# A third set of expert weights in the attention's matrices, list entries asked for three blocks ahead, half gathers behind half blocks

## The chip, the cores and the metric

The kernel runs on one core of one Trainium2 chip. A core has five engines with their own instruction streams: TensorE (PE, the matrix unit, with its weight loads PEld), VectorE (DVE), ScalarE (ACT), GpSimd (POOL) and SyncE (SP, which here issues most of the plain transfers). Sixteen DMA engines move data between the device memory and the on-chip memory. The metric is the device time of one execution in microseconds (us), as a median over several runs.

## The reference, cut to what matters

The input x has shape (4, 1024, 256): 4096 tokens of 256 features. Each token passes a gated scan layer (the "attention") and then a mixture of experts, both inside an adaptive layer norm. All data are float32.

```python
h = layernorm(x) * (1 + ca) + sa
x = x + ga * attn(h)            # K, u, g_in, g_out = sigmoid/linear parts of xn @ W_K, xn @ W_ugg;
                                # scan over the sequence; (outputs * g_out) @ W_out, plus h
h = layernorm(x) * (1 + cb) + sb
scores = top2(softmax(h @ Wg + bg))              # 8 experts, 2 per token, renormalised
for e in range(8):                               # W1[e]: 256 x 1024, W2[e]: 1024 x 256
    y = gelu(h @ W1[e] + b1[e]) @ W2[e] + b2[e]
    out += y * weight_of_expert_e
x = x + gb * out
```

## The kernel before

**First part, the attention.** The tokens go through in eight chunks of 512 (`for c_ in range(NCH)`). For each chunk `project` is called four times (`hc` 0 to 3); each call makes four products with slices of `wk_sb` and `wu_sb` (the tiles `pk`, `pgi`, `pu`, `pgo`, line 411). W_K, W_ugg and W_out lie in on-chip memory in the tiles `wk_sb`, `wu_sb` and `wo_sb` for the whole run. `wo_sb` is read by `scale_out` only, at the start of a sequence. Inside the last `project` call of the last chunk, between the products `pgi` and `pu`, stands `b_turn(0)`: PE turns the rows of the first expert block (tile `ptx`, line 878).

**The lists.** In between the chunks the gate's choices are sorted: for each token and chosen expert a pair (token, weight) is scattered into a list in device memory (`lists`, line 580). Each expert's list is cut into blocks of 256 tokens (`TK`); a table of block number to expert and place is computed on the chip: `tab["e"]` for the first eight blocks (`NE`), which are made from the first half of the tokens alone, and `tab["l"]` for the others. The blocks that have over 128 tokens ("whole") come first and those with at most 128 ("half") last. How many there are of either depends on the data, so the last blocks stand in branches: `n_whole` and `n_blocks` are read from the chip. In this run 36 blocks are used: 31 whole ones, then 5 half ones. In what follows they are named by their number: 30 is the last whole block, 31 to 35 are the half ones.

**Second part, the blocks.** For a block `j` the kernel does:

- `fetch_entries(j)`: SP reads the block's place from the table and loads its entries (`ente` for the first eight, `ent` in four turns for the others, 2 KB, line 808).
- `fetch_rows(j)`: POOL gathers the rows of the tokens from `hx` in device memory into `hb` (three turns), in two indirect transfers of 128 rows of 2 KB (line 820).
- `fetch_weights(j)`: SP loads `w1` (1 MB), `bb`, `w2` (1 MB) and `b2b` (128 KB) of the expert, in two turns each (lines 837 to 840).
- `b_turn(j)`: DVE turns `hb` into `xT` by sixteen 32-row transposes (line 885).
- `b_up(j)`: PE makes `ph` from `w1` and `xT` (line 898), ACT the gelu `g` (line 907).
- `b_down(j)`: PE makes `pye` from `g` and `w2` (line 928); DVE adds `b2b` and multiplies by weight and gate (lines 942, 943); POOL adds the result to the output in device memory by an indirect accumulating transfer (line 915).

From block 31 on the last result of a block is kept back: it goes to the one tile `last_y` with its places copied into the one tile `last_at` (line 938), and is sent by `add_rows` at the start of the next block's branch (`rest`, line 1160). So block j+1 may write `last_at` only when the transfer of block j has landed.

**The order.** It is written out by hand (`manual_schedule`): every engine runs its instructions in program order. `fetch(j)`, called at the start of block j, asks for the rows of block j+2 (and, from block 8 on, its entries just ahead of them) and for the weights of block j+1. `fetch_used(j)` does the same with a branch around each of the two, and stands ahead of the branch on `n_whole`. The first weights and all eight early entries are asked for in the last chunk:

```python
if not more:
    fetch_weights(0)
    for j in range(NE):
        fetch_entries(j)
    wait_for(BK[0]["ld"], scattered)
    fetch_rows(0)
    fetch_rows(1)
```

The weights of block 1 follow after the chunk loop, in `fetch(0)`.

Transfers that SP issues use eight completion counters in turn, and a transfer that takes a counter waits for the one that had it before.

Of the kernel before, what the change touches and what calls it, by code (L numbers as in the profile page):

```python
# [9 lines left out]
F32 = mybir.dt.float32  # L10
I32 = mybir.dt.int32
# [8 lines left out]
def tile_adaln_block(  # L20
# [33 lines left out]
    P = 128  # L54
    B, S, D = x.shape
    H = W_out.shape[0]
    E, _, F = W1.shape
    T = B * S
    KC = D // P
    HC = H // P  # L60
    FC = F // P
# [6 lines left out]
    HK = TK // P  # L68
# [5 lines left out]
    NJ = (2 * T + E * (TK - 1)) // TK  # L74
    BPE = T // TK
    NE = 8
# [13 lines left out]
    apool = ctx.enter_context(tc.tile_pool(name="attn", bufs=1))  # L90
# [3 lines left out]
    xpool = ctx.enter_context(tc.tile_pool(name="blocks", bufs=2))  # L94
# [11 lines left out]
        )  # L106
    )

    wk_sb = apool.tile([P, KC, H], F32, tag="wk", name="wk_sb")
    wu_sb = apool.tile([P, KC, 3 * H], F32, tag="wu", name="wu_sb")  # L110
    wo_sb = apool.tile([P, HC, D], F32, tag="wo", name="wo_sb")

    kts = [
# [120 lines left out]
    def a_norm(c_):  # L234
        X[c_]["h"] = deep.tile([P, TPB, D], F32, tag="h", name=f"h_{c_}")
        norm(X[c_]["h"], c_)
# [235 lines left out]
    def f_norm(c_):  # L472
        norm(new_h2(c_), c_)
# [301 lines left out]
    BK, tab = {}, {}  # L775
# [3 lines left out]
    def turns(pool, n: int, shape, dtype, tag: str, j: int):  # L779

        slots = kept.setdefault(tag, [None] * n)
        if slots[j % n] is None:
            slots[j % n] = pool.tile(shape, dtype, tag=f"{tag}{j % n}", name=f"{tag}_{j % n}", bufs=1)
        return slots[j % n]
# [6 lines left out]
    def seen(j: int):  # L791
        return EARLY_B * S if j < NE else T
# [8 lines left out]
    def fetch_entries(j: int):  # L801
        at = entry(j, 1, E * BPE)
        if j < NE:
            ent = xpool.tile([P, HK, 2], I32, tag=f"ente{j}", name=f"ente_{j}", bufs=1)
        else:
            ent = turns(xpool, 4, [P, HK, 2], I32, "ent", j)
        with nc.allow_non_contiguous_dma(reason="pairs of a list"):
            ld = nc.sync.dma_start(out=ent, in_=by_block[at])
        BK.setdefault(j, {}).update(ent=ent, ld=ld, gathers=[], acc=[])

    def fetch_rows(j: int):

        if j >= NJ:
            return
        if j >= NE:
            fetch_entries(j)
        hb = turns(xpool, 3, [P, HK, 2 * D], F32, "hb", j)
        for t in range(HK):
            BK[j]["gathers"].append(
                nc.gpsimd.indirect_dma_start(  # L820
                    out=hb[:, t, :], out_offset=None, in_=hx[: seen(j), :],
                    in_offset=IndirectOffsetOnAxis(ap=BK[j]["ent"][:, t, 0:1], axis=0),
                    bounds_check=seen(j) - 1, oob_is_err=False,
                )
            )
        BK[j]["hb"] = hb

    def fetch_weights(j: int):
        if j >= NJ:
            return  # L830
        wpool = pools["w"]
        e = entry(j, 0, E - 1)
        w1 = turns(wpool, 2, [P, KC, F], F32, "w1", j)
        w2 = turns(wpool, 2, [P, FC, D], F32, "w2", j)
        bb = turns(wpool, 2, [P, FC], F32, "bb", j)
        b2b = turns(wpool, 2, [P, D], F32, "b2b", j)
        nc.sync.dma_start(out=w1, in_=W1r[e])
        nc.sync.dma_start(out=bb, in_=b1d[e])
        nc.sync.dma_start(out=w2, in_=W2r[e])
        nc.sync.dma_start(out=b2b, in_=b2[ds(e, 1), :].broadcast_to((P, D)))  # L840
        BK.setdefault(j, {}).update(w1=w1, w2=w2, bb=bb, b2b=b2b)

    def fetch(j: int):

        fetch_rows(j + 2)
        fetch_weights(j + 1)

    def fetch_used(j: int):


        def used(i: int, step):
            if i < sure:
                step(i)
            elif i < NJ:
                with tc.If(n_blocks > i):
                    step(i)

        used(j + 2, fetch_rows)
        used(j + 1, fetch_weights)

    def wait_for(ins, others):
        for other in others:
# [3 lines left out]
                reason="all of it is there",  # L866
            )

    def b_turn(j: int):


        xT = turns(xpool, 2, [P, KC, TK], F32, "xT", j)
        BK[j]["xT"] = xT
        if j == 0:
            pt = ps_tr.tile([P, KC, TK], F32, tag="tr", name=f"ptx_{j}")
            for k in range(KC):
                for t in range(HK):
                    nc.tensor.transpose(pt[:, k, ts(t, P)], BK[j]["hb"][:, t, ts(k, P)], ident)
            nc.vector.tensor_copy(xT, pt)
            return  # L880
        hb = BK[j]["hb"][:, :, :D].rearrange("p t (k c) -> p t k c", k=KC)
        to = xT.rearrange("p k (t n) -> p t k n", t=HK)
        for i in range(NQ):
            for q in range(NQ):
                nc.vector.transpose(to[ts(q, SQ), :, :, ts(i, SQ)], hb[ts(i, SQ), :, :, ts(q, SQ)])  # L885
# [78 lines left out]
    h = X[0]["h"]  # L964
# [25 lines left out]
    for c_ in range(NCH):  # L990
        nxt, prv, old = c_ + 1, c_ - 1, c_ - 2
        more, was, been = nxt < NCH, prv >= 0, old >= 0
        b, part = divmod(c_, NB)

        route = old // NB if been and old % NB == NB - 1 else None
        placed = (c_ - 3) // NB if c_ >= 3 and (c_ - 3) % NB == NB - 1 else None


        if c_ + 3 < NCH:
            load_x(c_ + 3, nc.sync)  # L1000
        if more:
            shift(nxt)
        project(c_, 0, [lambda: a_norm(nxt)] if more else [])
        drain(6)
        if more:
            a_mod(nxt)
        if was:
            a_skip(c_)
            o_pe(prv)
            o_resid(prv)  # L1010
        if placed is not None:
            r_second(placed)
        if part == NB - 1:
            load_mdf(b + 1)


        if part == 0 and was:
            scale_out(b)
        if was:
            f_stats(prv)  # L1020
        project(c_, 1, [lambda: a_square(nxt)] if more else [])
        if c_ == 0:
            first_contents()
        drain(6)
        if placed is not None:
            r_rank_pe(placed)
        if been:
            f_gate(old)
        if not more:
            fetch_weights(0)  # L1030
            for j in range(NE):
                fetch_entries(j)

# [3 lines that stand above are left out]
        if part == 0:  # L1037
            if c_ == 0:
                setup_ctx.close()
                pools["w"] = ctx.enter_context(tc.tile_pool(name="weights", bufs=2))  # L1040
            load_gb(b)
            load_mda(b + 1)
        elif c_ == 1:
            clear_rows()
            if c_ == 0:
                load_mdf(1)


        if more:
            a_root(nxt)  # L1050
        if was:
            shift(prv)
        if placed is not None:
            r_place(placed)
        if route is not None:
            r_softmax(route)
        if more:
            a_scale(nxt)
        project(
            c_, 2,  # L1060
            ([lambda: f_norm(prv)] if was else [])
            + ([lambda: r_exp(route)] if route is not None else []),
        )
        drain(6)
        if part == 0:
            store_gb(b)
        if c_ + 2 < NCH:
            a_stats(c_ + 2)


        if not was:
            a_skip(c_)
            scale_out(b)
        if was:
            f_mod(prv)
            f_store(prv)
        project(c_, 3, [lambda: a_turn(nxt) if more else b_turn(0)])
        drain(6)
        if was:
            f_swap(prv)  # L1080
        if route is not None:
            r_first(route)
        if placed == EARLY_B - 1:
            tab["e"] = early_table()
# [35 lines left out]
    tab["l"], ends_at = late_table()  # L1120

    def work(j: int, half: bool = False, keep: bool = False):
        b_up(j, half)
        if j + 1 < NJ:
            b_turn(j + 1)
        b_down(j, half, keep=keep)

    def work_either(j: int, keep: bool = False):
# [6 lines left out]
    sure_whole = (2 * T - E * P) // TK  # L1135
    sure = 2 * T // TK
    for j in range(3, sure_whole):
# [14 lines left out]
    n_blocks = nc.values_load(  # L1152
        ends_at[0:1, 1:2], min_val=sure, max_val=NJ, skip_runtime_bounds_check_because=why
    )
    for j in range(sure_whole, sure):
        fetch_used(j)
        work_either(j, j == sure - 1)

    def rest(j: int):
        with tc.If(n_blocks > j):  # L1160
            add_rows(last_y, last_at, T)
            fetch_used(j)
            work_either(j, True)
            if j + 1 < NJ:
                rest(j + 1)
# [37 lines left out]
```

## Time and profile before

| | |
|---|---|
| median of 7 runs | 795.58 us (792.21 to 797.11) |
| profiled execution, own time | 793.5 us |
| its span, first to last instruction | 791.8 us |
| PE busy | 772.3 us (98%) |
| DVE, ACT, POOL busy | 507.1, 242.1, 296.5 us |
| granted PE clock | 0.997 |
| bytes moved | 138.11 MB, 174 GB/s over the span |
| up products of whole blocks, line 898 | 992 records, 219.3 us |
| down products of whole blocks, line 928 | 992 records, 219.5 us |

A whole block has 32 records of each product, so 992 are 31 blocks. The profile's own time is 1.7 us above its span; the median of the runs is 2.08 us above the profiled execution. "Busy" of PE is modelled and holds no waiting; the gaps of PE are read from the timeline, where a bracket after an instruction says how long the engine had been idle before it and what ended that.

### The profile page before, as it was taken

How to read it: one execution, taken by the hardware profiler on the slowest of the kernel's cores; microseconds unless marked ns; L12 is line 12 of the kernel's file. 1: busy time of each engine (PE TensorE's matmuls, PEld its weight loads, DVE VectorE, ACT ScalarE, POOL GpSimd, SP SyncE). 2: the span in 40 equal slices, each digit the busy share in tenths (PEclk: the TensorE clock that was granted, in tenths of full speed). 3: DMA queues.
4: the chain of work that ended last, by engine and by line, in shares of the span. 5: the costliest groups of instructions: out<-in, count | busy, mean ns of one | idle time of the engine just before them, and what ended most of it. 6: DMA issues, size and time to landing. Idle time of an engine off the chain costs nothing.

```text
span 791.8 us, 10818 instructions
## 1 busy us (share of the span) xinstructions
PE 772.3 (98%) x3279; PEld 576.7 (73%) x3279; DVE 507.1 (64%) x1369; ACT 242.1 (31%) x560; POOL 296.5 (37%) x372
## 2 busy tenths in 40 slices
PE   8999999999999999999999999999999999999983
PEld 4464545464555647888888888888888888888973
DVE  5787877899789968778453545445363544536554
ACT  4434243535353242322132222213122221312221
POOL 2103010107302830788843424334342433434431
PEclk9999999999999999999999999999999999999998
DMA  8311434052322367789797777778787777867592
GB/s 294 108 55 48 133 100 126 27 174 56 79 80 87 81 181 237 183 230 225 181 286 227 215 210 218 225 211 240 210 220 218 211 217 217 241 185 214 170 300 60
DMA packets 115462, 138.11 MB, mean 174 GB/s; under 512 B 25206, under 2 KB 99514, under 8 KB 115392
## 3 DMA queue, kind: packets, MB, share of 16 engines
q1 hardware_dynamic: 96368, 111.45, 46.1%
q0 software_dynamic: 17456, 25.25, 14.4%
q10 hardware_dynamic: 1568, 0.57, 0.3%
q8 instruction: 32, 0.52, 0.3%
q14 instruction: 38, 0.31, 0.1%
HBM read 114.31 MB, written 25.42 MB: 176 GB/s over the span
## 4 chain that ended last, share of the span: by engine, by line
PE 90%; DMA 5%; DVE 2%; SPq 1%; issue 1%; POOLq 0%; POOL 0%; ACT 0%; DVEq 0%
PE pye_False L928 26%; PE ph_False L898 26%; PE pya L448 7%; PE pu L411 7%; PE pk L411 6%; PE pgi L411 6%; PE pgo L411 6%; DMA hb<-hx,ent 3%; PE idle L257 1%; DMA w<-in_L_ffn_W_dram 1%; PE pta L393 1%; PE pm L284 1%; PE ph_True L898 1%; DMA ent<-lists 1%; DMA hb<-hx,ente 1%
## 5 line engine op out<-in xcount | busy, mean ns | idle before, releaser
L928 PE MATMUL pye_False<-w,g_False 128*128 128x256 f32 x992 | 219.5, 379 | 0.0
L898 PE MATMUL ph_False<-xT,w 128*128 128x256 f32 x992 | 219.3, 379 | 0.0
L898 PEld LDWEIGHTS ph_False<-xT,w 128*128 128x128 f32 x992 | 188.3, 190 | 26.3 <-issue 0.5
L928 PEld LDWEIGHTS pye_False<-w,g_False 128*128 128x128 f32 x992 | 188.2, 190 | 25.9 <-issue 0.2
L907 ACT ACTIVATE g_False<-ph_False,bb 128x256 f32<-128x256 f32 x248 | 104.0, 471 | 301.2 <-issue 197.5
L885 DVE STREAM_TRANSPOSE xT<-hb 32x128 f32<-32x128 f32 x576 | 174.2, 302 | 19.0 <-DMA hb<-hx,ent 6.6
L942 DVE TENSOR_TENSOR yb_False<-pye_False,b2b 128x256 f32<-128x256 f32 x62 | 26.3, 424 | 186.5 <-PE pye_False L928 186.4
L915 POOL DMA_INDIRECT out_dram<-yb_False,ent x46 | 73.8, 1604 | 178.5 <-DVE yb_False L943 178.5
L580 POOL DMA_INDIRECT lists<-pay,placei x64 | 66.6, 1040 | 12.5 <-issue 11.3
L820 POOL DMA_INDIRECT hb<-hx,ent x56 | 59.0, 1053 | 20.5 <-issue 16.2
L411 PE MATMUL pk<-hT,wk_sb 128*128 128x512 f32 x128 | 61.0, 599 | 0.7 <-ACT hT L985 0.7
L411 PE MATMUL pu<-hT,wu_sb 128*128 128x512 f32 x128 | 60.2, 592 | 0.0
L411 PE MATMUL pgi<-hT,wu_sb 128*128 128x512 f32 x128 | 60.1, 592 | 0.0
L411 PE MATMUL pgo<-hT,wu_sb 128*128 128x512 f32 x128 | 60.1, 592 | 0.0
L448 PE MATMUL pya<-wo,z 128*128 128x256 f32 x256 | 56.6, 379 | 0.0
L217 POOL TENSOR_TENSOR rstd_f<-rstd_f,expo 128x4 f32<-128x4 f32 x8 | 8.2, 1019 | 128.0 <-DVE rstd_f L216 128.0
L448 PEld LDWEIGHTS pya<-wo,z 128*128 128x128 f32 x256 | 48.6, 190 | 9.5 <-issue 3.3
L411 PEld LDWEIGHTS pgi<-hT,wu_sb 128*128 128x128 f32 x128 | 24.3, 190 | 30.6 <-issue 30.4
L411 PEld LDWEIGHTS pgo<-hT,wu_sb 128*128 128x128 f32 x128 | 24.3, 190 | 30.6 <-issue 26.8
L421 ACT ACTIVATE kt<-pk 128x512 f32<-128x512 f32 x32 | 19.2, 599 | 82.4 <-PE pk L411 82.4
L411 PEld LDWEIGHTS pu<-hT,wu_sb 128*128 128x128 f32 x128 | 23.7, 190 | 26.8 <-issue 24.6
L411 PEld LDWEIGHTS pk<-hT,wk_sb 128*128 128x128 f32 x128 | 23.7, 190 | 26.0 <-issue 23.0
(195 smaller groups left out, 691.2 us busy)
## 6 DMA issues: line engine op xcount, KB each, us to landing
w<-in_L_ffn_W_dram SPq DMA_DIRECT2D x72, 1024.0 KB
b2b<-in_L_ffn_b_dram SPq DMA_DIRECT2D x36, 128.0 KB
hx<-gb SPq DMA_DIRECT2D x4, 1024.0 KB
out_dram<-x SPq DMA_DIRECT2D x8, 512.0 KB
hx<-h SPq DMA_DIRECT2D x8, 512.0 KB
x<-in_L_attn_x_dram SPq DMA_DIRECT2D x7, 512.0 KB
swapped<-u SPq DMA_DIRECT2D x7, 512.0 KB
hT<-swapped SPq DMA_DIRECT2D x28, 128.0 KB
```

What stands on the lines that cost most here:

```text
L217: nc.gpsimd.tensor_tensor(rstd, rstd, expo[:, 0, :], ALU.pow)
L411: nc.tensor.matmul(ps, lhsT=w[:, k, col : col + P], rhs=hT[:, k, :], start=(k == 0), stop=(k == KC - 1),)
L421: nc.scalar.activation(kt[:, 1:], ps, AF.Sigmoid)
L448: nc.tensor.matmul(py[:, t, :], lhsT=z[hc][:, ts(2 * q + t, P)], rhs=wo[:, hc, :], start=(hc == 0), stop=(hc == HC - 1),)
L580: ins = nc.gpsimd.indirect_dma_start(out=lists[:, :], out_offset=IndirectOffsetOnAxis(ap=place, axis=0), in_=what, in_offset=None, bounds_ ...
L820: nc.gpsimd.indirect_dma_start(out=hb[:, t, :], out_offset=None, in_=hx[: seen(j), :], in_offset=IndirectOffsetOnAxis(ap=BK[j]["ent"][:, t ...
L885: nc.vector.transpose(to[ts(q, SQ), :, :, ts(i, SQ)], hb[ts(i, SQ), :, :, ts(q, SQ)])
L898: nc.tensor.matmul(ph[:, u, :], lhsT=w1[:, k, ts(fc, P)], rhs=xT[:, k, :n], start=(k == 0), stop=(k == KC - 1),)
L907: nc.scalar.activation(g[:, fc, :n], ph[:, u, :], AF.Gelu_apprx_tanh, bias=bb[:, fc : fc + 1])
L915: return nc.gpsimd.indirect_dma_start(out=out_rows[:n], out_offset=IndirectOffsetOnAxis(ap=at, axis=0), in_=yb, in_offset=None, bounds_che ...
L928: nc.tensor.matmul(py, lhsT=g[:, fc, ts(t, P)], rhs=w2[:, fc, :], start=(fc == 0), stop=(fc == FC - 1),)
L942: nc.vector.tensor_add(yb, py, b2b)
```

## The change

W_K and W_ugg get one tile, `proj`, of 4096 columns; `wk_sb` and `wu_sb` become views of it. Each block whose number leaves rest 2 when divided by 3 takes its weights from there: `w1` and `w2` in the two halves of `proj`, `b2b` in the first quarter of `wo_sb`. The others use the two old sets, so there are three sets, and three turns of `bb`. Weights are asked for at the start of block j for block j+2 instead of j+1; in the last chunk the weights of block 1 are asked for right behind those of block 0, ahead of the eight early entries. Entries of the late blocks are asked for at block j for j+3, in five turns instead of four, and without a branch. In a half block, one gather instead of two is made for block j+2 and the transposes for block j+1 take only the first 128 rows. `fetch_used` moves into the two branches of `work_either`, and its two inner branches become one.

```diff
-    wk_sb = apool.tile([P, KC, H], F32, tag="wk", name="wk_sb")
-    wu_sb = apool.tile([P, KC, 3 * H], F32, tag="wu", name="wu_sb")
+    proj = apool.tile([P, 4 * KC * H], F32, tag="proj", name="proj")
+    wk_sb = proj[:, : KC * H].rearrange("p (k h) -> p k h", k=KC)
+    wu_sb = proj[:, KC * H :].rearrange("p (k h) -> p k h", k=KC)
...
-            ent = turns(xpool, 4, [P, HK, 2], I32, "ent", j)
+            ent = turns(xpool, 5, [P, HK, 2], I32, "ent", j)
...
-    def fetch_rows(j: int):
-        if j >= NJ:
-            return
-        if j >= NE:
-            fetch_entries(j)
+    def fetch_rows(j: int, half: bool = False):
         hb = turns(xpool, 3, [P, HK, 2 * D], F32, "hb", j)
-        for t in range(HK):
+        for t in range(1 if half else HK):
...
-        w1 = turns(wpool, 2, [P, KC, F], F32, "w1", j)
-        w2 = turns(wpool, 2, [P, FC, D], F32, "w2", j)
-        bb = turns(wpool, 2, [P, FC], F32, "bb", j)
-        b2b = turns(wpool, 2, [P, D], F32, "b2b", j)
+        if j % 3 == 2:
+            w1 = proj[:, : KC * F].rearrange("p (k f) -> p k f", k=KC)
+            w2 = proj[:, KC * F :].rearrange("p (c d) -> p c d", c=FC)
+            b2b = wo_sb[:, 0, :]
+        else:
+            w1 = turns(wpool, 2, [P, KC, F], F32, "w1", j % 3)
+            w2 = turns(wpool, 2, [P, FC, D], F32, "w2", j % 3)
+            b2b = turns(wpool, 2, [P, D], F32, "b2b", j % 3)
+        bb = turns(wpool, 3, [P, FC], F32, "bb", j)
...
+    firsts = (NE,)
     def fetch(j: int):
-        fetch_rows(j + 2)
-        fetch_weights(j + 1)
-    def fetch_used(j: int):
-        def used(i: int, step):
-            if i < sure:
-                step(i)
-            elif i < NJ:
-                with tc.If(n_blocks > i):
-                    step(i)
-        used(j + 2, fetch_rows)
-        used(j + 1, fetch_weights)
+        if j + 2 in firsts:
+            fetch_entries(j + 2)
+        if NE < j + 3 < NJ and j + 3 not in firsts:
+            fetch_entries(j + 3)
+        if j + 2 < NJ:
+            fetch_rows(j + 2)
+            fetch_weights(j + 2)
+    def fetch_used(j: int, half: bool):
+        if j + 3 < NJ:
+            fetch_entries(j + 3)
+        def rest():
+            fetch_rows(j + 2, half)
+            fetch_weights(j + 2)
+        if j + 2 < sure:
+            rest()
+        elif j + 2 < NJ:
+            with tc.If(n_blocks > j + 2):
+                rest()
...
-    def b_turn(j: int):
+    def b_turn(j: int, half: bool = False):
...
-        hb = BK[j]["hb"][:, :, :D].rearrange("p t (k c) -> p t k c", k=KC)
-        to = xT.rearrange("p k (t n) -> p t k n", t=HK)
+        n_t = 1 if half else HK
+        hb = BK[j]["hb"][:, :n_t, :D].rearrange("p t (k c) -> p t k c", k=KC)
+        to = xT.rearrange("p k (t n) -> p t k n", t=HK)[:, :n_t]
...
             fetch_weights(0)
+            fetch_weights(1)
             for j in range(NE):
                 fetch_entries(j)
...
     def work(j: int, half: bool = False, keep: bool = False):
+        if j >= sure_whole:
+            fetch_used(j, half)
         b_up(j, half)
         if j + 1 < NJ:
-            b_turn(j + 1)
+            b_turn(j + 1, half)
...
     for j in range(sure_whole, sure):
-        fetch_used(j)
         work_either(j, j == sure - 1)
...
             add_rows(last_y, last_at, T)
-            fetch_used(j)
             work_either(j, True)
```

## The prediction

> **What bounds the kernel now.** The page comes first: PE is busy for 98% of the span and is 90% of the chain that ended last, so only gaps of PE can be won, and every new gap of PE costs in full. The second view, busy times by stretch, shows where gaps are.
>
> ```profile
> PE 90%; DMA 5%; DVE 2%; SPq 1%; issue 1%; POOLq 0%; POOL 0%; ACT 0%; DVEq 0%
> ...
> 281.25:287.25 6.00, 6.00 (x30) 2.65 (x29) 4.25 (x9) 1.20 (x2) 0.00 (x0) 1.00 1.00 344
> ...
> 600.00:700.00 100.00, 100.00 (x465) 88.03 (x464) 46.91 (x142) 23.52 (x56) 39.62 (x38) 1.00 0.78 220
> 700.00:740.00 40.00, 40.00 (x188) 35.22 (x187) 18.98 (x58) 10.08 (x24) 16.16 (x15) 1.00 0.67 189
> 740.00:770.00 30.00, 27.16 (x186) 24.95 (x185) 19.00 (x61) 9.15 (x32) 12.64 (x10) 1.00 0.84 266
> ```
>
> The second column is PE's busy time. The whole blocks, to 740, have no gap: there the third set can win nothing. Gaps lie among the five half blocks. The third view is PE's timeline there.
>
> ```profile
> 739.87 3.73 PE L898 MATMUL ph_True<-xT,w 128*128 128x128 f32 x32
> ...
> 746.94 3.73 PE L898 MATMUL ph_True<-xT,w 128*128 128x128 f32 x32
> ...
> 755.52 3.81 PE L898 MATMUL ph_True<-xT,w 128*128 128x128 f32 x32 [1.39 <-DMA w<-in_L_ffn_W_dram]
> 760.11 3.69 PE L928 MATMUL pye_True<-w,g_True 128*128 128x256 f32 x16 [0.79 <-ACT g_True L907]
> ...
> 768.03 3.69 PE L928 MATMUL pye_True<-w,g_True 128*128 128x256 f32 x16 [0.66 <-ACT g_True L907]
> 774.73 3.81 PE L898 MATMUL ph_True<-xT,w 128*128 128x128 f32 x32 [3.01 <-DVE xT L885]
> 778.38 3.62 PE L928 MATMUL pye_True<-w,g_True 128*128 128x256 f32 x16
> ```
>
> Block 31 takes 746.94 - 739.87 = 7.07 us without a gap. Five would take 35.35; they take 782.00 - 739.87 = 42.13. So 6.8 us is the most that the end can give. The fourth view is the place that the change touches early: the timeline of the last chunk, all engines.
>
> ```profile
> 278.53 0.41 SPq L837 DMA_DIRECT2D w<-in_L_ffn_W_dram  x1
> ...
> 281.97 7.73 SPq L808 DMA_DIRECT2D ente<-lists  x8
> ...
> 289.94 1.10 POOL L820 DMA_INDIRECT hb<-hx,ente  x1 [9.65 <-DMA ente<-lists]
> ...
> 291.35 1.75 POOL L820 DMA_INDIRECT hb<-hx,ente  x1 [0.31 <-issue]
> ...
> 295.42 0.55 PE L878 MATMUL ptx<-ident,hb 128*128 128x128 f32 x3 [0.73 <-DMA hb<-hx,ente]
> ```
>
> The first entries are issued at 281.97 and POOL has them at 289.94, 8 us later; the last of the eight, issued at 289.3 when nothing is ahead, lands in 3.5. In 281.25 to 287.25 the DMA engines are 100% busy with block 0's weights at 344 GB/s, and in the 2.75 us after it move 33 GB/s. So the small entry load stands behind 2 MB of weights. And PE waits for its result: the turn of block 0 stands in PE's order between two products, and already has a gap of 0.73.
>
> **Part 1, block 1's weights ahead of the entries (a cost).** SP's four issues and the table read take 281.97 - 278.53 = 3.44 us, so the first entry is issued at 285.4 or, since it takes over the completion counter of the first `w1`, a little later. Ahead of it now stand another 2.10 + 0.13 MB. At 344 GB/s that is 6.5 us: the queue drains at 293.7 instead of 287.25, the entries land at 296.4, the gathers are issued at 296.4 and 297.8, the second lands after the 4.03 us of the chain of waits (291.35 to 295.38), at 301.9, and PE goes on 6.5 us later than before. Nothing hides it: PE is in order, `pu`, `pgo` and block 0 stand behind the turn, and DVE's and SP's later work follows them. Bounds: if the entries were let past the weights and only the issue were later, they would land at 285.4 + 3.5 = 288.9, at no cost; if they kept the 7.97 us of before, +3.4; if the gather takes the longest landing of these six, 6.3 instead of 4.0, +8.8. I take 6.5, by the row of the weights that now stand there already.
>
> [...]
>
> **Part 2, block 2's weights into `proj`.** SP issues them where block 1's went (307.80), and they now wait for the last product `pgo`, which ends before that. Behind them on SP are the last chunk's stores, as before. Block 2 uses them at 353. Cost 0. The pieces of `proj` are loaded and read by their own regions in the order of before, so the start is unchanged.
>
> **Part 3, whole blocks.** The same bytes, the same free slots at the same moments, one block earlier relative to their use; PE's gap there is 0 before and can only stay 0.
>
> **Part 4, the end (a gain).** Weights of 32 are now asked for during block 30, of 33 at 740, of 34 at about 748.7 (the entries ahead of them wait for block 30's last add, as the issue at 747.51 shows) and of 35 from about 755, when `w1` of 34 has landed and frees SP's counter. All 2.23 MB sets at 344 GB/s take 6.5 us: 34 is there by 757 and needed at 761; 35 by about 764 and needed at 768 (`w1`) and 771.7 (`w2`). So the 1.39 goes, and so do the 0.79 and 0.66: gelu was done there in time (in blocks 31 and 35 the same order shows no wait), and what came late was `w2`, issued at 750.35 and 761.03.
>
> The 3.01 is the rows of block 35:
>
> ```profile
> 755.53 0.37 SPq L808 DMA_DIRECT2D ent<-lists  x1
> ...
> 755.94 0.15 DVE L938 COPY last_at<-ent 128x1 int32<-128x1 int32 x1 [2.43 <-DMA out_dram<-last_y,last_at]
> ...
> 761.34 1.05 POOL L820 DMA_INDIRECT hb<-hx,ent  x1 [2.46 <-DMA ent<-lists]
> ```
>
> Their entries were asked for at 755.53 and kept POOL waiting till 761.34. Now they are asked for at about 747.5, and POOL gathers right after block 32's add, at 757.3 + 1.6 + 0.3 = 759.2. The one half gather lands in 4.6 to 7.9 us (those of the end): 763.8 to 767.1, say 765.7. The sixteen transposes take 5.06 us; a half one has 64 columns instead of 128. From 303 ns for 128 and 1240 ns for 1024 (line 508) it is some 235 ns, 4.0 us in all (bounds: half of 5.06, and 5.06). So `xT` of 35 is ready at 769.7, where PE could start at 768.2: 1.5 us remains of the 3.01 and its refill. The gain is 6.8 - 1.5 = 5.3, between 4.0 (gather 7.9, transposes 5.06, or adds that land late) and 6.8.
>
> The branches: one inner branch less on PE, DVE and ACT; SP's program grows from 591 to 705 rows, POOL's from 460 to 483. PE crosses from block 31 to 32 at its full pitch of 7.07 with two such branches, so I take 0. After the last product 792 - 782 = 10 us follow unchanged.
>
> [...]
>
> **Sum.** +6.5 - 5.3 = +1.2. On the profiled execution's 793.5 (span 791.8 and 1.7 around it) that is 794.7 us; on the median, 2.08 above that execution, 796.8. About 0.3% (2.4 us) is what a measurement of this kernel can tell from no change, so this is no change that can be told, on the slow side.
>
> **Rivals.**
>
> *The kept-back adds become the bound of the end (slower).* `last_at` and `last_y` are single: each half block must wait till the add of the one before has landed. The row at 755.94 shows it, and the issues at 748.33 and 757.28 give the period: 8.95 us, of which 7.6 is the landing and 1.35 DVE and POOL. Four periods of that lead to 784.1, later than 783.34 before: no gain. The forecast's end, 783.34 - 5.3 = 778.0 before the early shift, is a mean period of 7.4, so a mean landing of 6.1; from 6.4 on the gain is under 4.1 and the change counts as slower. For it: landings of 7.6 and 7.4 under load. Against it: with the weights in by 764, the last two adds have the queues alone, like the last one of before, 3.6. If it decides, the gain is 2 to 3 and the time 795.6 + 6.5 - 2.5 = 799.6.
>
> *The weights do not hold the entries (faster).* Part 1 costs 0 to 3.4: 795.6 - 5.3 = 790.3 to 793.7. For it: the 8 us are one case only. Against it: the landing ends 2.7 us after the busy stretch, and the entries of 755.53 likewise land, at 760.6, when the `w2` ahead of them lets PE go on (760.11).
>
> *The end stays bound by bytes, the third set doing nothing there.* 266 GB/s in 740 to 770 is 84% of DMA time. With no gain: 795.6 + 6.5 = 802.1. Against it: the block ahead is filled while whole blocks run at 67%.
>
> **Chances.** Forecast 0.50 (its own range 794 to 798.4), adds bound 0.20, entries not held 0.15, no gain 0.08; the remaining 0.07 is an early cost of 8.8 with the forecast's end, 799.1. Faster by over 0.3%: nearly all of the entries rival, 0.14. Slower: adds, no gain, the longer gap and a little of the forecast, 0.38. Within: 0.48. The range leaves out half of the entries rival and most of the no-gain one: 792.0 to 801.0.
>
> **What would show it.** Right: a gap of about 7 us at the turn of block 0, with the first entries landing near 296; no wait for weights after 740; a gap of about 1.5 or less before block 35; the last product ending about 1 us later than 782. Wrong: the turn's gap under 4, gathers kept from POOL by entries at the end, copies of `last_at` idle on an add in blocks 33 to 35, or any gap between 330 and 740.

## The result and the profile after

The changed kernel takes 796.74 us in the median of 26 runs (795.24 to 798.73), the kernel before 794.47 us in 62 runs (791.27 to 798.42). The ratio is 1.0027, 95% interval 1.0018 to 1.0036: some 2 us slower, about the bound of what a measurement of this kernel can tell. The profiled execution has a span of 794.2 us, 2.4 more than before.

So the time hardly moved, and the two halves of the change moved it by 9 and by 7 us in opposite directions. In the page of the changed kernel the chain that ended last now has more DMA and less PE:

```profile
PE 83%; DMA 9%; DVE 2%; issue 2%; SPq 2%; POOL 0%; POOLq 0%; ACT 0%; DVEq 0%
```

The first half is the turn of block 0. From the timeline of the changed kernel (start, duration, engine and line), SP, POOL and PE:

```profile
283.45 5.02 SPq L843 DMA_DIRECT2D b2b<-in_L_ffn_b_dram  x1
289.24 6.59 SPq L810 DMA_DIRECT2D ente<-lists  x8
...
295.95 2.02 POOL L818 DMA_INDIRECT hb<-hx,ente  x1 [15.55 <-DMA ente<-lists]
...
301.99 1.46 PE L891 MATMUL ptx<-ident,hb 128*128 128x128 f32 x4 [7.32 <-DMA hb<-hx,ente]
303.25 3.62 PE L413 MATMUL pu<-hT,proj 128*128 128x512 f32 x4
306.66 2.03 PE L413 MATMUL pgo<-hT,proj 128*128 128x512 f32 x4
308.53 7.07 PE L912 MATMUL ph_False<-xT,w 128*128 128x256 f32 x32
```

POOL gets its entries at 295.95 instead of 289.94, and PE goes on at 301.99 instead of 295.42, 6.57 us later. Then `pu` takes 3.62 us. In the timeline of the kernel before, the same four products take 1.88, and block 0 starts at 299.24 instead of 308.53:

```profile
295.81 1.88 PE L411 MATMUL pu<-hT,wu_sb 128*128 128x512 f32 x4
...
299.24 7.07 PE L898 MATMUL ph_False<-xT,w 128*128 128x256 f32 x32
```

That is 9.29 us, of which 2.72 are no wait at all. The busy times by stretch of the changed kernel say what they are (after the stretch and its length come PE, PEld, DVE, ACT and POOL busy; then the granted PE clock, the DMA share and GB/s):

```profile
296.00:297.00 1.00, 0.00 (x0) 0.00 (x0) 1.00 (x1) 0.00 (x0) 1.00 (x1) 0.86 0.15 2
297.00:298.00 1.00, 0.00 (x0) 0.00 (x0) 0.00 (x0) 0.00 (x0) 0.97 (x1) 0.50 0.02 7
...
303.25:306.66 3.41, 3.41 (x5) 1.35 (x5) 0.69 (x1) 0.00 (x0) 1.01 (x1) 0.50 0.72 214
306.66:308.50 1.84, 1.84 (x5) 0.91 (x4) 1.45 (x3) 0.00 (x0) 0.00 (x0) 0.92 0.04 11
```

PE had stopped at 294.68. While it stands the granted clock falls to 0.50, at about 296.7, and it is 1.00 again only from about 307.0, some 5 us after the first product at 301.99.

The second half is the end. The timeline of PE in the changed kernel, half blocks 31, 34 and 35:

```profile
749.06 3.73 PE L912 MATMUL ph_True<-xT,w 128*128 128x128 f32 x32
...
770.15 3.81 PE L912 MATMUL ph_True<-xT,w 128*128 128x128 f32 x32
...
777.25 3.74 PE L912 MATMUL ph_True<-xT,proj 128*128 128x128 f32 x32
780.83 3.62 PE L942 MATMUL pye_True<-proj,g_True 128*128 128x256 f32 x16
```

No bracket is left. The five half blocks take 784.45 - 749.06 = 35.39 us, for 42.13 before: a gain of 6.74. From the start of block 0 to that of block 31 only 0.10 us changes (440.53 us for 440.63). So the last product ends 9.29 - 0.10 - 6.74 = 2.45 us later than before, and the last add too (785.79 for 783.34).

That PE has no gap does not mean that nothing is close behind it. The timeline of DVE in the changed kernel:

```profile
763.99 0.16 DVE L952 COPY last_at<-ent 128x1 int32<-128x1 int32 x1 [2.68 <-DMA out_dram<-last_y,last_at]
...
766.05 4.00 DVE L899 STREAM_TRANSPOSE xT<-hb 32x64 f32<-32x64 f32 x16 [1.01 <-DMA hb<-hx,ent]
...
771.66 0.15 DVE L952 COPY last_at<-ent 128x1 int32<-128x1 int32 x1 [1.61 <-DMA out_dram<-last_y,last_at]
```

DVE waits for the kept-back adds, and the transposes of block 34 wait for its rows. They end at 770.05, and PE takes them up at 770.15.

### The profile page after: what moved, and what is told of

The parts are those of the page before. It is cut to its first block, busy times and chain, and to the rows that moved or that the text cites. A ratio compares the mean times of both kernels' runs of the same rounds, so it can differ in the third digit from the quotient of the medians.

```text
span 794.2 us, 10783 instructions
## 1 busy us (share of the span) xinstructions
PE 773.9 (97%) x3279; PEld 578.4 (73%) x3279; DVE 501.9 (63%) x1369; ACT 241.8 (30%) x560; POOL 293.8 (37%) x369
## 4 chain that ended last, share of the span: by engine, by line
PE 83%; DMA 9%; DVE 2%; issue 2%; SPq 2%; POOL 0%; POOLq 0%; ACT 0%; DVEq 0%
PE pye_False L942 24%; PE ph_False L912 24%; DMA hb<-hx,ent 7%; PE pya L450 7%; PE pu L413 7%; PE pk L413 6%; PE pgo L413 6%; PE pgi L413 6%; PE idle L259 1%; DMA out_dram<-yb_False,ent 1%; SPq L843 1%; PE pta L395 1%; PE pm L286 1%; DMA hb<-hx,ente 1%; PE pl L560 0%
## 5 line engine op out<-in xcount | busy, mean ns | idle before, releaser
L899 DVE STREAM_TRANSPOSE xT<-hb 32x128 f32<-32x128 f32 (+1 forms) x576 | 168.9, 293 | 11.4 <-DMA hb<-hx,ente 1.3
L942 PE MATMUL pye_False<-w,g_False 128*128 128x256 f32 x672 | 148.7, 379 | 0.0
L912 PE MATMUL ph_False<-xT,w 128*128 128x256 f32 x672 | 148.6, 379 | 0.0
L912 PEld LDWEIGHTS ph_False<-xT,w 128*128 128x128 f32 x672 | 127.6, 190 | 18.0 <-issue 0.5
L942 PE MATMUL pye_False<-proj,g_False 128*128 128x256 f32 x320 | 70.8, 379 | 0.0
L912 PE MATMUL ph_False<-xT,proj 128*128 128x256 f32 x320 | 70.7, 379 | 0.0
L912 PEld LDWEIGHTS ph_False<-xT,proj 128*128 128x128 f32 x320 | 60.8, 190 | 8.3
L942 PEld LDWEIGHTS pye_False<-proj,g_False 128*128 128x128 f32 x320 | 60.7, 190 | 8.2
L413 PE MATMUL pu<-hT,proj 128*128 128x512 f32 x128 | 61.9, 607 | 0.0
L413 PE MATMUL pk<-hT,proj 128*128 128x512 f32 x128 | 61.0, 599 | 0.7 <-ACT hT L999 0.7
```

The costliest lines, as they stand in the source:

```text
L413: nc.tensor.matmul(ps, lhsT=w[:, k, col : col + P], rhs=hT[:, k, :], start=(k == 0), stop=(k == KC - 1),)
L912: nc.tensor.matmul(ph[:, u, :], lhsT=w1[:, k, ts(fc, P)], rhs=xT[:, k, :n], start=(k == 0), stop=(k == KC - 1),)
L942: nc.tensor.matmul(py, lhsT=g[:, fc, ts(t, P)], rhs=w2[:, fc, :], start=(fc == 0), stop=(fc == FC - 1),)
```

## The experiments

"End" is the time from the start of block 31 to the end of the last product. Each ratio is to runs of the kernel before on the same chip; on the three chips these had medians of 793.75, 794.89 and 810.51 us.

**The second set asked for later.** Everything of the change but the early order:

```diff
-            fetch_weights(1)      # ahead of the eight early entries
...
     last = NCH - 1
+    fetch_weights(1)
     fetch(0)
```

> The changed kernel with one call moved: the weights of block 1 are asked for after the chunk loop, where the kernel before asked for them, no longer ahead of the eight early entries; all else of the change stays. Theory (the early order costs 9.3 us: 6.6 that the rows of block 0 land later and 2.7 in which the PE clock is halved after the gap; the end gives 6.7): the gap at the turn of block 0 is 0.7 again, the clock stays 1.00, the five half blocks keep their pitch of 7.07 without a gap, and the time is 794.5 - 6.7 = 787.8, ratio 0.992. Rival 1 (the lead over the weights that is won early is what fills the end; without it the end waits again): gaps of 2 or more after 740, 790 to 794. Rival 2 (two sets of weights asked for back to back after the loop hold up the stores and row gathers of blocks 1 and 2): new gaps of PE between 310 and 350, 790 or more.

Measured: 788.77 us (788.24 to 789.67), ratio 0.9939 [0.9923, 0.9956]. The timeline of PE in this kernel:

```profile
296.22 0.55 PE L891 MATMUL ptx<-ident,hb 128*128 128x128 f32 x3 [0.79 <-DMA hb<-hx,ente]
...
763.04 3.81 PE L912 MATMUL ph_True<-xT,w 128*128 128x128 f32 x32 [1.14 <-issue]
```

The turn has about its old gap (0.79 for 0.73), `pu` takes 1.88 again, and no gap comes up later for want of block 1's weights. Block 0 starts 8.5 us earlier than in the changed kernel. The time falls by 7 us and not by 8.5, since the end takes 36.68 instead of 35.39: PE now stands 1.14 us ahead of block 34, which the theory did not have. It is not the weights of rival 1 that it waits for: DVE gets block 34's rows at 758.95 and has them turned at 762.95. This version is faster than both kernels.

**The early order alone**, in the kernel before:

```diff
         fetch_rows(j + 2)
-        fetch_weights(j + 1)
+        if j > 0:
+            fetch_weights(j + 1)
...
             fetch_weights(0)
+            fetch_weights(1)
```

> The kernel before with one call moved: the weights of block 1 are asked for behind those of block 0, ahead of the eight early entries, as in the changed kernel; two sets, entries and rows as before. Theory: the whole early cost and nothing else, 9.3 us with the halved clock: 794.5 + 9.3 = 803.8, ratio 1.012, and the end with its gaps of 5.9 as before. Rival (the slow products behind the gap belong to something else in the changed kernel, such as its one tile for all four matrices): the clock stays at 1.00 and the cost is the later landing alone, 6.6: 801.1, ratio 1.008.

Measured: 804.29 us (803.16 to 807.60), ratio 1.0145 [1.0117, 1.0172]. The timeline of PE in this kernel:

```profile
301.85 1.45 PE L879 MATMUL ptx<-ident,hb 128*128 128x128 f32 x4 [7.26 <-DMA hb<-hx,ente]
303.09 3.62 PE L411 MATMUL pu<-hT,wu_sb 128*128 128x512 f32 x4
```

The same 7.3 and the same 3.62 stand in a kernel that has nothing else of the change. Block 0 starts at 308.37, 9.13 later than before. With the experiment above, the early order costs some 9 us at block 0 from either side (8.5 and 9.13). The time rises by more, 10.5 us, because the end of the profiled execution takes 43.60 us for 42.13.

**The stand filled.** The changed kernel with 58 transposes of the identity ahead of the turn, into a PSUM tile that nobody reads; their only use is that PE works:

```diff
+            spare = ps_y.tile([P, TB], F32, tag="y", name="spare")
+            for _ in range(58):
+                nc.tensor.transpose(spare[:, :P], ident, ident)
             pt = ps_tr.tile([P, KC, TK], F32, tag="tr", name=f"ptx_{j}")
```

> The changed kernel with 58 turns of a constant square put on PE ahead of the turn of block 0 (0.12 us each, 7.0 us in all, as the idle turns at the start), so that PE works where it waited; their result is not used. Theory (the clock is granted by recent work: after the 7.3 us gap it was 0.50 from 297 to 307, and the products pu and pgo took 5.4 instead of 3.4): the clock stays at 1.00, pu takes 1.88 again, the rows land as late as before, and the time is 796.7 - 2.7 = 794.0, within 0.3% of the kernel before. Rival (the products are slow for their operands or for the transfers beside them): pu still takes 3.6, 796.7 or more.

Measured: 795.84 us (793.73 to 798.58), ratio 1.0024 [1.0007, 1.0041], the same as the changed kernel. By the time alone the theory fell. The timeline of PE in this kernel:

```profile
294.77 6.49 PE L890 MATMUL spare<-ident 128*128 128x128 f32 x58
...
303.36 1.88 PE L413 MATMUL pu<-hT,proj 128*128 128x512 f32 x4
...
770.34 3.81 PE L915 MATMUL ph_True<-xT,w 128*128 128x128 f32 x32 [1.47 <-issue]
```

The clock stays at 1.00 through 296 to 309, `pu` has its 1.88 back, and block 0 starts at 306.79, 1.74 us earlier than in the changed kernel. That is the mechanism, shown. The 1.74 is then lost where the set-back kernel lost its own: block 34 begins at 770.34, in the changed kernel at 770.15. What is ahead of it there came early, block 34's rows did not: POOL's queue stood ahead of them till an add of block 30 had landed (below, at part 4). In the profiled executions, PE's earlier time ends at that point.

**Half of the filling**, 30 transposes, one run.

```diff
-            for _ in range(58):
+            for _ in range(30):
```

> As the kernel with the filled gap, with 30 turns instead of 58: PE works for the first 3.6 us of the wait and stands for the last 3.7 or so. A look at how long a gap may be: in the kernel before, 3.0 us at 771.7 left the clock at 1.00, and 7.3 halved it. If a gap of 3.7 is still short enough, pu takes 1.88 and the clock stays at 1.00 up to 310; if not, the clock is 0.50 from 299 or 300 on and pu takes up to 3.6.

Measured: 798.02 us. PE stands 1.68 us, does one transpose of 0.30, and stands 3.34 more (timeline of PE):

```profile
303.91 0.90 PE L894 MATMUL ptx<-ident,hb 128*128 128x128 f32 x3 [3.34 <-DMA hb<-hx,ente]
304.61 3.07 PE L413 MATMUL pu<-hT,proj 128*128 128x512 f32 x4
```

The clock falls inside that stretch (0.59 in 303 to 306), and `pu` takes 3.07. One product of 0.30 us did not hold the clock over these 5.02 us of standing.

**What of the change wins the end?** Three variants of the set-back kernel, each with one part of the change undone. First, all rows and full transposes behind half blocks:

```diff
-        for t in range(1 if half else HK):
+        for t in range(HK):
...
-        n_t = 1 if half else HK
+        n_t = HK
```

> Set back (block 1's weights asked for behind the early entries), but both gathers and full transposes behind half blocks again. Theory: the half rows are what keeps the last stands small. A second gather (1.03 us and 0.31 of issue) puts the rows' landing back by 1.34 us, a full transpose takes 5.05 us for 4.00, so the 1.14 us that TensorE stands ahead of block 34 grow to about 3.5 us: 791.3 us against a before of 793.75, ratio 0.997. Rival: the rows that aren't gathered were hidden behind the adds' landings anyway, and the time stays that of the set-back kernel, 788.8 us, ratio 0.994.

Measured: 791.63 us (789.41 to 795.98), ratio 0.9963 [0.9944, 0.9981], as the theory had it. The stand is shared out otherwise than expected: 1.53 us ahead of block 34 and 1.54 ahead of block 35, and the end takes 39.07 us, 2.39 more than with half rows.

Second, weights one block ahead:

```diff
-            fetch_weights(j + 2)
+        if j + 1 < NJ:
+            fetch_weights(j + 1)
...
-        def rest():
-            fetch_rows(j + 2, half)
-            fetch_weights(j + 2)
+        used(j + 2, lambda i: fetch_rows(i, half))
+        used(j + 1, fetch_weights)
```

> The changed kernel with each block's weights asked for one block ahead as in the kernel before, three sets kept, entries three blocks ahead, half rows kept; so nothing stands ahead of the early entries. Theory: the third set's whole worth is that the weights are asked for a block earlier; without it the waits of 1.39, 0.79 and 0.66 us behind the half blocks come back (2.84 in all), less the 1.14 us that the set-back kernel stands ahead of block 34 in any case, if both fall on the same blocks: 790.5 to 791.6 us against a before of 793.75, ratio 0.996 to 0.997. Rival: with fewer rows to bring in, the weights land in time at one block ahead: 788.8 us, ratio 0.994.

Measured: 791.83 us (789.50 to 795.21), ratio 0.9965 [0.9948, 0.9982]. The size is as expected, but its place is not: in the profiled execution PE waits for no weights, and the last product ends 36.59 us after block 31 began, as in the set-back kernel. The loss comes behind it. The timeline of POOL in this kernel:

```profile
772.77 1.56 POOL L930 DMA_INDIRECT out_dram<-last_y,last_at  x1 [6.42 <-DVE last_y L958]
780.53 1.55 POOL L930 DMA_INDIRECT out_dram<-last_y,last_at  x1 [6.20 <-issue]
```

The last add is issued 4.39 us after the last product, for 1.34 in the set-back kernel. Copies of `last_at` wait for the add before in four blocks, 9.7 us in all. Weights asked for a block later load while the kept-back adds should land: the DMA engines move 336 GB/s in 765 to 770, for 186 in the set-back kernel. From block 31 to the last add it is 40.98 us for 38.02. So here the kept-back adds do bound the end. That PE waits for no weights is what the rival said: in this profile they are in time without being asked for early.

Third, entries two blocks ahead instead of three:

```diff
-        if NE < j + 3 < NJ and j + 3 not in firsts:
-            fetch_entries(j + 3)
...
-        if j + 3 < NJ:
-            fetch_entries(j + 3)
+        if j + 2 < NJ:
+            fetch_entries(j + 2)
```

> Set back, but entries asked for only two blocks ahead, as in the kernel before. Theory: the gathers of a block are issued as soon as its entries are there, and asked for together the gather waits for the entry's landing, some 2 us; that moves block 34's and 35's rows back by as much, and the stand ahead of block 34 grows from 1.14 to about 3 us: 790.5 us against a before of 793.75, ratio 0.996. Rival: GpSimd waits for the landing of the add ahead of the gather longer than for the entry (5.46 us in the set-back kernel), so the third block of advance is worth nothing: 788.8 us, ratio 0.994.

Measured: 789.13 us (788.99 to 790.74), ratio 0.9926 [0.9902, 0.9950]: the rival. Once half rows and the third set are there, the third block of advance for the entries has no worth that these runs can tell. The profiled execution, the slowest of the six (the others take 788.99 to 789.32), does have a long end, 39.43 us. The timeline of PE there, at block 33:

```profile
756.50 5.44 PE L910 MATMUL ph_True<-xT,w 128*128 128x128 f32 x32 [2.27 <-issue]
```

The entries are not the cause: the gather of block 33's rows is issued 3.32 us after block 31 began, in the set-back kernel 3.33. But it is issued at 743.33, and DVE gets the rows at 752.40, 9.1 us later. Behind this stand of 2.27 us the clock was 0.50 (from 757.4 to 760.8), and the product took 5.44 us, 1.6 more than the 3.81 of the one that follows the stand of 1.14 us at a clock of 1.00 in the set-back kernel.

**The rows ahead of the kept-back add**, at the first block that has one. In the set-back kernel GpSimd waits 5.46 us for the landing of the add before, and block 34's gather is queued behind that add.

```diff
         if j >= sure_whole:
             fetch_used(j, half)
+        if j == sure:
+            add_rows(last_y, last_at, T)
...
-            add_rows(last_y, last_at, T)
+            if j > sure:
+                add_rows(last_y, last_at, T)
```

> Set back, and at the first block whose add was kept back the rows of two blocks on are gathered ahead of that add instead of behind it. Theory: the stand of 1.14 us ahead of block 34 is GpSimd's queue: the add waits 5.46 us for the landing of the add before it, the gather of block 34's rows is queued behind it, and its rows land at 758.95 in the profile of the set-back kernel, 1.1 us too late. With the gather first they land near 756, the transposes begin once the sum of block 32 is done (757.9), and the stand falls to 0.1 or less: 787.7 us against a before of 793.75, ratio 0.9925. Rival: the add is what counts; it is put off by the gather, each kept-back sum behind it lands later, and the stand moves to block 35: 788.8 us or more, ratio 0.994 or above.

Measured: 791.09 us (789.55 to 795.08), ratio 0.9953 [0.9937, 0.9969]: no gain, as the rival had it. (The set-back kernel itself was not run on this chip; the kernel with entries two ahead was, with 0.9926.) The profiled execution is the slowest of its runs, 4 us above their median. The timeline of DVE there:

```profile
757.68 0.15 DVE L952 COPY last_at<-ent 128x1 int32<-128x1 int32 x1 [4.70 <-DMA out_dram<-last_y,last_at]
...
770.53 4.00 DVE L899 STREAM_TRANSPOSE xT<-hb 32x64 f32<-32x64 f32 x16 [3.52 <-DMA hb<-hx,ent]
```

Block 34's rows are there in time now, but its transposes stand on DVE behind block 32's sum, and that waits till 757.68 for an add to land. Product 34 starts at 762.92, for 763.04 without the edit. Block 35 then waits for rows that were asked for at 760.90 and came at 770.5, and PE stands 4.35 us ahead of it; in the set-back kernel block 35's gather took at most 5.3 us and block 34's 6.5. Why this one took 9.6 stays open: in 765 to 770 the DMA engines are busy for only 49%.

**The set-back kernel once more, and two ways to better it.** These four ran on one chip. The first is unchanged:

> The set-back kernel once more, beside the next three on one chip, since they are to differ from it by 0.1 to 0.3 per cent: ratio 0.994 to before, as measured (0.9923 to 0.9956).

Measured: 804.01 us (802.25 to 805.65), ratio 0.9916 [0.9891, 0.9942], with an end of 37.17 us. On this chip every kernel was slower, the one before too (810.51), and the four profiles show one more stand, in 361 to 376, where PE, ScalarE and VectorE all work in pieces; so only ratios are compared. Even these are to be read with care: PE stands there for 12.0 us in this profile and for 7.9 to 8.8 in the three below, so a part of what they seem to gain may be this.

Entries 0 and 1 ahead of block 0's weights:

```diff
+            for j in range(2):
+                fetch_entries(j)
             fetch_weights(0)
-            for j in range(NE):
+            for j in range(2, NE):
                 fetch_entries(j)
```

> Set back, and entries 0 and 1 asked for ahead of block 0's weights as well. Theory: in the set-back kernel TensorE still stands 0.79 us for block 0's second rows, since its entries are queued behind 2 MB of block 0's weights; with entries 0 and 1 first the rows are there, and block 0's weights, asked for 0.8 us later, still land before block 0 needs them (299.9): 0.8 us less than the set-back kernel, ratio 0.993. Rival: block 0's weights or the rows wait for something else than the queue (the lists written just before): same as the set-back kernel, 0.994.

Measured: 802.35 us (796.09 to 805.54), ratio 0.9898 [0.9860, 0.9937]. The first gather starts at 282.68, for 289.17 in the next kernel, so it was the queue and not the lists that the entries waited for. The turn has no gap in the profiled execution. But the next kernel, without this edit, has none there either, so no gain of time is shown by that.

Two buffers for the kept-back sum, and rows first in each half block:

```diff
-                yb, at = last_y, last_at
-                nc.vector.tensor_copy(last_at, ent[:, t, 0:1])
+                yb, at = last_y[j % 2], last_at[j % 2]
+                nc.vector.tensor_copy(at, ent[:, t, 0:1])
...
             fetch_used(j, half)
+        if j >= sure:
+            add_last(j - 1)
...
-        with tc.If(n_blocks > j):
-            add_rows(last_y, last_at, T)
+        with tc.If(n_blocks > j) as more:
             work_either(j, True)
...
+        with more.Else():
+            add_last(j - 1)
```

> Set back, with two buffers in turn for the kept-back sum and its tokens, and each half block's rows gathered ahead of the add that was kept back (the final add moves into the branches' ends, its work is the same). Theory: the end is bound by the kept-back adds: VectorE waits for an add's landing (2.67 us in the set-back kernel, 4.70 and 3.14 in the one with the rows first) before it writes the next sum, and the next transposes are queued behind that sum. With two buffers no sum waits, the five half blocks take TensorE's own 35.2 to 35.4 us for 36.68, and only the adds' order among themselves is left, some 6 to 7.5 us each beside 7.03 of TensorE: 1.3 us less than the set-back kernel, 787.5 us against a before of 793.75, ratio 0.992, and less spread between runs. Rival: the rows' landing is what binds (6.5 to 9.5 us behind a block's weights in the same engines), the buffers change nothing: ratio 0.994 and the same spread.

Measured: 802.36 us (796.71 to 803.92), ratio 0.9894 [0.9860, 0.9928]. In the profiled execution the end takes 35.29 us, and no copy of `last_at` waits for an add. It is the adds that wait for each other (timeline of POOL):

```profile
785.76 1.55 POOL L929 DMA_INDIRECT out_dram<-last_y,last_at  x1 [5.12 <-DMA out_dram<-wo_sb,last_at]
```

Here `wo_sb` holds the second buffer. The runs do not spread less than those of the set-back kernel on this chip (7.2 us for 3.4). Both edits in one kernel:

> Both of these: entries 0 and 1 ahead of block 0's weights, and two buffers for the kept-back sum with the rows first. If both theories hold the gains add, 0.8 and 1.3 us below the set-back kernel: 786.7 us against a before of 793.75, ratio 0.991. If only one does, 0.992 to 0.993; if neither, 0.994.

Measured: 801.53 us (795.72 to 802.99), ratio 0.9882 [0.9848, 0.9915], with an end of 35.30 us. It has the lowest ratio of all and its steps are as meant in its trace. But the intervals of the four overlap, and the kernel with entries first had an end of 35.32 without the second buffer: in that profile the adds landed in time anyway. So it is the best candidate, and its 0.3% over the set-back kernel is not proven.

## Why the prediction was right, and where its steps were wrong

It said 796.8 us, +1.2 by its sum; the medians show 796.74 and +2.27, the profiles +2.45. The change is close because two errors of opposite sign stand in it: the early cost was 2.8 us too small and the gain at the end 1.4 too small. That the time meets to 0.1 us is luck on top of that: the sum stands on the 795.58 of 7 runs, the 62 runs beside the changed kernel give 794.47, and this 1.1 makes up for the 1.1 that +1.2 lacks.

*Part 1, the entries behind the weights: right, with one step missing.* Forecast 6.5 us later, measured 6.57. The queue works as read from the row of 344 GB/s: 354 GB/s in 287.25 to 293.75, entries at 295.95 (forecast 296.4). The issue was not at 285.4 but at 289.24, because SP was held in one issue for 5.02 us; as the queue was the bound, that cost nothing. The rival "the weights do not hold the entries" is out: let past, entries issued at 289.24 would have landed at 292.7, after 3.5 us. The step that failed is "PE goes on 6.5 us later than before": it took every product behind the gap at its old duration. The halved clock adds 0.87 on `ptx`, 1.70 on `pu` and 0.15 on `pgo`, 2.72 in all, and the kernel with the early order alone shows the same. The profile of before had the row for it, where PE stops for good (granted clock in the column before the last two):

```profile
787.00:788.00 1.00, 0.00 (x0) 0.00 (x0) 0.00 (x0) 0.00 (x0) 0.00 (x0) 0.67 0.00 0
```

PE ended at 782.0 there and the clock fell 5.3 us later, while the stand of 3.01 us at 771.7 left it at 1.00. A forecast of a 7 us stand should have had a term for that. Its size could not be worked out from that profile: the clock falls only this once there and does not come back, and in the changed kernel it fell 2.0 us after PE stopped at 294.68, not 5.3, and came back 5.0 us after the first product. Measured are the 2.72.

*Parts 2 and 3: right.* No wait for `proj` shows, and from block 0 to block 31 the changed kernel is within 0.10 us of before.

*Part 4, the end: right that the waits go, only partly right about what removes them, too small by 1.4 us.* Forecast gain 5.3, measured 6.74, the most that was there being 6.8. The three waits for weights are gone. They are gone too in the kernel that asks for weights one block ahead, so the early asking was not needed for that. The 1.5 us kept of the 3.01 is gone too, and that is the term that was mis-sized. In the set-back kernel a rest of the stand is left, ahead of block 34 instead of 35, and the gain is 42.13 - 36.68 = 5.45. The other 1.3 us hang on one landing. Block 31 starts 8.4 us later in the changed kernel than in the set-back one, but counted from there POOL's instructions agree to 0.02 us in both up to block 33's gather. Then POOL comes to the first kept-back add. Its timeline in the changed kernel:

```profile
757.53 1.59 POOL L929 DMA_INDIRECT out_dram<-last_y,last_at  x1 [4.06 <-DVE last_y L957]
```

and in the set-back one:

```profile
750.53 1.59 POOL L929 DMA_INDIRECT out_dram<-last_y,last_at  x1 [5.46 <-DMA out_dram<-yb_False,ent]
```

Block 30's last add was issued 7.04 us ahead of the first row (750.49) and had landed; it was issued 8.44 us ahead of the second (742.09), which waits for it, and block 34's gather stands behind. In the filled kernel it is 9.03 us, with the same wait, and in the set-back kernel on the third chip 7.31, without it. So the landing differs from one execution to another, of one kernel too, and that the late start helps it is not shown. The half transposes measure 4.00 us against the estimate of 4.0. The half rows are worth 2.39 us in the end, by the kernel with full rows (its ratio is 0.9963 for 0.9939); the weights asked for two blocks ahead are worth 2.96 us up to the last add (0.9965 for 0.9939), but in that kernel's profile all of it lies in the adds' landings, which the forecast did not connect with the weights. The third block of advance for the entries, to which the forecast gave the cure of the 3.01, shows no worth of its own in the medians.

*The rival of the kept-back adds* was the nearest one. It decides from a mean landing of 6.4; the first two take 6.4 and 6.3, the next at most 4.6 and 3.8. So it did not decide in the changed kernel's profile. In those of the set-back and the filled kernel, and where the weights load later, rows and adds set the end, and 1 to 3 us go there. That "copies of `last_at` idle on an add" would show the forecast wrong was too strict: they do idle, by 1.61 and 0.54 in blocks 33 and 34 (2.68 in block 32), and PE has no gap.

*No gain at the end because of bytes:* out, by the 6.74.

## What to carry to other kernels

A small transfer that an engine in order waits for belongs ahead of large ones on its queue: here 2 MB of weights asked for earlier than anybody needed them brought the entries at 295.95 instead of 289.94 and took back all that the rest of the change won. A gap on PE can cost more than its length, as the products behind it took longer in these runs: 2.72 us more behind a stand of 7.3, where the granted clock was 0.50, 1.6 more behind stands of 2.27 and 4.35, nothing behind one of 3.0; price both. And when one wait at the end is removed, look at the engine beside it: the next bound, rows and adds, lay within 0.1 us in the changed kernel's profile, and one late landing was enough to reach it in others. One profile of a kernel does not tell such landings from the effect of an edit.

## What the runs showed of the hardware

- The clock fell 2.0 us after PE stopped in the changed kernel (294.68 to about 296.7) and 5.4 us after in the kernel with the early order alone (294.59 to about 300.0), at the same place with the same stand of 7.3 us. It came back about 5 us after PE's first product in both (4.97 and 4.93).
- Read from rows of 1 us, the granted clock was 0.50 for 10.24 us in the changed kernel (296.72 to 306.96), 6.84 with the early order alone, 3.40 with half of the filling, and 3.42 in the kernels with entries two ahead and with the rows first: close to three times, twice and once 3.41 us. Of the 3.41 us before the fall PE had been busy for 40% in the changed kernel, and for 0, 9, 33 and 22% in these others, in the order named. In the kernel before it was busy for 12% of the 3.41 us up to the end of the stand of 3.01, and the clock stayed at 1.00. So in these traces neither the length of a stand nor this share decides alone: 2.27 us halved the clock, and 3.01 did not. What decides is not shown.
- An issue of a DMA on SP's queue took 5.02 us in the changed kernel, for the last of the eight transfers, 4.5 MB of weights, that are asked for in a row. The same line takes 0.39 us in the median there, but 3.08 at 336.99, and 6.27 at 348.28 with the early order alone; so it is not these eight alone, and the cause stays open.
- Landings of rows scatter: gathers of 128 rows at the end took 6.5 and 6.6 us in the profiles of the set-back and the changed kernel (block 34), 9.1 in that of entries two ahead and 9.6 in that of the rows first. That this makes the spread between runs (789.55 to 795.08 there, 788.24 to 789.67 of the set-back kernel) is the author's guess, and wasn't tried by itself.
- On the third chip all four profiled kernels have a stretch at 361 to 376 in which several engines work in pieces, PE stands for 7.9 to 12.0 us in all, and the clock falls with it (0.50 in 376 to 380 with two buffers, 0.54 in the set-back kernel). It is in no profile from the other chips; its cause stays open.
